# A graph layer with gathered sums: two matrices for u, later first slots, and a reload of node numbers set apart

## The chip, the cores and the metric

The kernel runs on one core of a Trainium2 chip. The metric is the device time of one launch in microseconds (us), lower is better. A core has five engines with a queue of instructions each: TensorE (PE, matmuls, with its weight loads shown as PEld), VectorE (DVE), ScalarE (ACT), GpSimd (POOL) and SyncE (SP, here used to start DMAs). Each engine works through its queue in order and waits on semaphores for the others. ACT, POOL and SP start DMAs, which run on the core's 16 DMA engines.

## The reference

A relational graph layer on N = 1250 nodes with D = 1024 features, E = 20000 edges of R = 8 types, with a normalization before it and a gate behind it:

```python
h = jnp.maximum(_layernorm(x, axis=-1), 0.0)
# u = _rgcn(h, edge_index, edge_type, weight, root, bias):
msgs = h[src]
out = h @ root + bias
for r in range(8):
    mask = (edge_type == r).astype(h.dtype)
    sums = jax.ops.segment_sum(msgs * mask[:, None], dst, num_segments=n)
    cnt = jax.ops.segment_sum(mask, dst, num_segments=n)
    mean = sums / jnp.maximum(cnt, 1.0)[:, None]
    out = out + mean @ weight[r]
u = out
z = jnp.concatenate([u, h], axis=1) @ w_gate + b_gate
out = x + jnp.tanh(u) * z + h * (1.0 - z)
```

## The kernel before

**The order of the mathematics.** The kernel multiplies first and sums over edges afterwards: for every edge type r it computes y_r = h @ weight[r] and writes it to DRAM. A node's u is then a weighted sum of rows of y, one row per incoming edge, the weight being one over the count of that node's edges of that type.

**TensorE's work.** Eleven matrices stand in the list `mats`: the eight weights, `root`, and the two halves of `w_gate`. `steps` runs over (s, i): s is the matrix, i one of five pairs of 128-row blocks of nodes (`NP` = 5, `ND` = 10 blocks). A step multiplies a pair of blocks with a matrix by Strassen's scheme (Winograd's form), so that seven products take the place of eight: function `product` (L270) with `step` (L361). From s = 1 on, one of the products of pairs 0 to 3 is itself taken apart once more (class `Second`, L178; its matmuls are the 128x256 ones of L209). The products' results are moved out of PSUM by ACT (copies, L303 to L337) and DVE (additions, L296, L304, L240), into `row` tiles of which there are four; SP stores the finished rows (L379), which frees the tile.

**Work beside the products.** After each of the seven products `product` calls `between(j)`. There a generator of other work is moved on: the function `spread` (L1058) deals `total` calls of a generator evenly over `parts` places, and `beside` (L1099) runs the steps up to matrix `last` with such a generator beside them. All engines' queues are in the order in which this Python code issues instructions; nothing reorders them afterwards. A DVE instruction of the side work thus stands in DVE's queue ahead of the row additions of the next product.

**Three groups of edges.** The types are cut in three groups, `R0 = (0, 3, 6, 8)`. Group g's sums begin when its y matrices (`y[g]`) are complete, and run beside two later matrices: group one beside s = 4 and 5, group two beside 6 and 7, group three beside 8 (`root`) and 9. In each group the nodes are sorted by their count of edges, and cut in ten blocks d of 128; `K[g][d]` says how many edges ("slots") the block's nodes have at most: 75, 75 and 52 slots per group. The sorted order is kept in `node[:, g, d]` (node numbers), and `idx[:, g, d, k]` is the row of y that slot k takes.

**One slot** is `add_slot` (L1003): POOL gathers 128 rows of y by `idx` into one of four `got` tiles (L1006), and DVE adds them, weighted, to the block's tile u (L1014; L1012 for the first slot of group one).

**One group** is the generator `edges` (L1026). `new_u` (L1018) makes a block's tile u; from the second group on it gathers u's state out of the DRAM matrix `u_dram` by node number (L462), because the groups have different orders. The tile of the next block is made at the second slot of the present one, after the finished block before it has been handed to `to`. For groups one and two `to` is `u_back` (L1051), which scatters u into `u_dram` by node number (`to_rows`, L466 to L471; the scatters of one group are declared independent of each other, as their rows differ). For group three it is a store to `last_dram` by SP (L1207), and for its last four blocks (`held`, L1281) u stays in SBUF. There is one matrix `u_dram`; a gather from it waits until every scatter into it that was issued earlier has landed.

**Node numbers of a group** come from `rows_and_weights` (L496): ten scatters of 4-byte values to `node_dram[g]` (L499), a reload of them as `node[:, g]` (L508), the keys `node_key` by a POOL addition (L509), and ten gathers of `idx` rows by key (L462). For group one it runs at once; for groups two and three it is a generator (`other_groups`, L1112) moved on at every second call of group one's slots. `weights(g)` computes the slots' weights on DVE (L486 to L491) after that.

**Overflow.** Nodes with more edges than slots are handled in a branch that these inputs do not enter: `passes_needed` (L1073) computes the flag beside group two, all engines load it (L1144) and branch (L1146) between the second and the third group.

Of the kernel before, what the change touches and what calls it, by code (L numbers as in the profile page):

```python
# [9 lines left out]
F32 = mybir.dt.float32  # L10
# [3 lines left out]
OP = mybir.AluOpType  # L14
# [5 lines left out]
def tile_rgcn_highway(  # L20
# [31 lines left out]
    nc = tc.nc  # L52
# [4 lines left out]
    N, D = x.shape  # L57
# [6 lines left out]
    ND = -(-N // P)  # L64
    NP = ND // 2
    NCH = -(-E // P)
    EL = E - (NCH - 1) * P
    G = 3
    R0 = (0, 3, 6, R)
# [5 lines left out]
    KEYS = ND * P  # L75
# [2 lines left out]
    FAR = 1 << 20  # L78
    CG = 4
    GOT = 4  # L80

    A11, A12, A22, S1, S2, S3, S4 = range(7)
    A21 = S3
# [17 lines left out]
    psum = ctx.enter_context(tc.tile_pool(name="psum", bufs=1, space=bass.MemoryType.PSUM))  # L101

    h_dram = dram.tile([N, D], F32, name="h_dram")
    u_dram = dram.tile([N, D], F32, name="u_dram")
    hr_dram = dram.tile([N, D], F32, name="hr_dram")
    z_dram = dram.tile([N, D], F32, name="z_dram")
    xh_dram = dram.tile([N, D], F32, name="xh_dram")
# [352 lines left out]
    def rows_of(to, of, at):  # L460

        nc.gpsimd.indirect_dma_start(  # L462
            out=to, out_offset=None, in_=of,
            in_offset=bass.IndirectOffsetOnAxis(ap=at, axis=0))

    def to_rows(of, frm, at, group):  # L466
        nc.gpsimd.memset(apart, 0.0)
        ins = nc.gpsimd.indirect_dma_start(  # L468
            out=of, out_offset=bass.IndirectOffsetOnAxis(ap=at, axis=0), in_=frm, in_offset=None)
        tc.declare_no_dep(ins.ins, query=no_wait, group=group, reason="rows differ")  # L470
        tc.add_to_no_dep_group(group, ins.ins)  # L471
# [24 lines left out]
    def rows_and_weights(g):  # L496

        for d in range(ND):
            ins = nc.gpsimd.indirect_dma_start(  # L499
                out=node_dram[g][:, :],  # L500
                out_offset=bass.IndirectOffsetOnAxis(ap=pos_i[:, g, d:d + 1], axis=0),
                in_=ids[:, d:d + 1], in_offset=None,
                bounds_check=KEYS - 1, oob_is_err=False)
            tc.declare_no_dep(ins.ins, query=no_wait, group="nodes", reason="places differ")
            tc.add_to_no_dep_group("nodes", ins.ins)
            if d % 2:
                yield
        nc.gpsimd.dma_start(node[:, g, :], node_dram[g].rearrange("(d p) o -> p (d o)", p=P))  # L508
        nc.gpsimd.tensor_single_scalar(node_key[:, g, :], node[:, g, :], g * KEYS, op=OP.add)  # L509
        yield  # L510
        yield
        for d in range(ND):
            rows_of(idx[:, g, d, :], table_rows, node_key[:, g, d:d + 1])
            if d % 2:
                yield

    with ExitStack() as early:
# [20 lines left out]
        class Normed:  # L538
# [13 lines left out]
            def spread(self):  # L552
                n = self.n
                nc.vector.bn_aggr(self.mv[:n], self.st[:n].rearrange("p a b -> p (a b)"))
                nc.scalar.activation(self.sd[:n], self.mv[:n, 1:2], AF.Sqrt, bias=eps[:n])
# [425 lines left out]
    with ExitStack() as edges_part:  # L981
# [41 lines left out]
                rows_of(u[:n], of[:, :], node[:n, g, d:d + 1])  # L1023
            return u

        def edges(g, blocks, to):  # L1026


            of = u_dram if g else None
            ahead = new_u(blocks[0], of, g)  # L1030
            behind = []

            def leave():
                while behind:
                    to(*behind.pop())

            for d in blocks:
                u = ahead
                last = K[g][d] - 1
                for k in range(last + 1):  # L1040
                    add_slot(u, g, d, k, idx[:, g], w_of[:, g], first=g == 0 and k == 0)
                    if k == min(1, last):
                        leave()
                        if d != blocks[-1]:
                            ahead = new_u(d + 1, of, g)
                    yield
                behind.append((d, u))
            leave()
            yield

        def u_back(g):  # L1051
            def to(d, u):
                n = nrows(d)
                to_rows(u_dram[:, :], u[:n], node[:n, g, d:d + 1], f"u{g}")

            return to

# [41 lines left out]
        def beside(e, total, s, i, last):  # L1099


            between = spread(e, total, 7 * ((last - s) * NP + NP - i))
            while s <= last:
                step(s, i, between)
                s, i = next(steps, (NM, 0))
            return s, i
# [26 lines left out]
        def with_passes(e):  # L1133
            passes = passes_needed()
            for _ in e:
                next(passes, None)
                yield

        for g in range(1, G - 1):
            e = edges(g, range(ND), u_back(g))  # L1140
            s, i = beside(with_passes(e) if g == G - 2 else e, sum(K[g]) + 1, s, i, R0[g + 2] - 1)


        passes = nc.values_load(n_pass[0:1, 0:1], min_val=0, max_val=E // MORE,  # L1144
# [1 line left out]
        with tc.If(passes > 0):  # L1146
            def further(g, d, ks, at, w):
                n = nrows(d)
                u = upool.tile([P, D], F32, name="u")
                rows_of(u[:n], u_dram[:, :], node[:n, g, d:d + 1])  # L1150
                for k in ks:
                    add_slot(u, g, d, k, at, w)
                nc.gpsimd.indirect_dma_start(
                    out=u_dram[:, :],
                    out_offset=bass.IndirectOffsetOnAxis(ap=node[:n, g, d:d + 1], axis=0),
                    in_=u[:n], in_offset=None)

            for g in range(G):
                for d in range(ND):
                    if K[g][d] < SLOTS:  # L1160
                        further(g, d, range(K[g][d], SLOTS), idx[:, g], w_of[:, g])
            scratch = got()
            used = [0]

            def part_of(n):
                used[0] += n
                return scratch[:, used[0] - n:used[0]]

            done = rank
            nc.vector.tensor_single_scalar(done, rank, float(-SLOTS), op=OP.add)  # L1170
            far_more = part_of(G * ND * MORE).bitcast(I32)
            nc.gpsimd.memset(far_more, FAR)
            under, where, where_i = part_of(NCH), part_of(NCH), part_of(NCH).bitcast(I32)
            at_more = part_of(ND * MORE).bitcast(I32).rearrange("p (d k) -> p d k", k=MORE)
            w_more, t_more = [part_of(ND * MORE).rearrange("p (d k) -> p d k", k=MORE)
                              for _ in range(2)]
            with tc.For_i(0, passes, 1):
                nc.gpsimd.dma_start(table_more.rearrange("(p f) o -> p (f o)", p=P), far_more)
                nc.vector.tensor_single_scalar(under, done, 0.0, op=OP.is_lt)
                nc.vector.tensor_single_scalar(where, done, float(MORE), op=OP.is_ge)  # L1180
                nc.vector.tensor_add(under, under, where)
                nc.vector.scalar_tensor_tensor(where, key_col, float(MORE), done,
                                               op0=OP.mult, op1=OP.add)
                nc.vector.scalar_tensor_tensor(where, under, float(FAR), where,
                                               op0=OP.mult, op1=OP.add)
                nc.vector.tensor_scalar_max(where_i, where, 0.0)
                for c in range(NCH):
                    n = nedges(c)
                    nc.gpsimd.indirect_dma_start(
                        out=table_more[:, :],  # L1190
                        out_offset=bass.IndirectOffsetOnAxis(ap=where_i[:n, c:c + 1], axis=0),
                        in_=row_col[:n, c:c + 1], in_offset=None,
                        bounds_check=G * KEYS * MORE - 1, oob_is_err=False)
                for g in range(G):
                    slot_rows(g, more_rows, at_more)
                    slot_weights(g, at_more, w_more, t_more, drc)
                    for d in range(ND):
                        further(g, d, range(MORE), at_more, w_more)
                nc.vector.tensor_single_scalar(done, done, float(-MORE), op=OP.add)
# [16 lines left out]
        def in_turn(*es):  # L1216
            for e in es:
                yield from e
# [62 lines left out]
        def held():  # L1281

            new, old = [], []
            for _ in edges(LG, range(HELD), lambda d, u: new.append(add_hr(d, u))):
                yield
                for add in old:
                    add()
                old, new[:] = new[:], []
            for add in old + new:
                add()  # L1290

        late = edges(LG, range(HELD, ND), to_last)
        between = spread(in_turn(late, held()), sum(K[LG]) + 2, 7 * ((NM - 2 - s) * NP + NP - i))
        while s < NM - 1:
            def beside_h(j):
                between(j)
# [69 lines left out]
```

## Time and profile before

| | |
|---|---|
| Median of 3 runs | 1399.93 us (1399.35 to 1403.1) |
| The profiled execution's own time | 1399.42 us |
| Its span | 1397.6 us |
| DVE L1014, slot additions | 192 of 1282 ns, 245.7 us |
| POOL L1006, slot gathers | 202 of 1238 ns, 250.2 us |
| POOL L468, scatters to u_dram | 20, median 1035 ns |
| POOL L462, gathers from u_dram | 20, median 957 ns |
| DMA queue of POOL's indirect transfers | 128.60 MB, 30.0% of 16 engines |
| TensorE's mean granted clock | 0.99 |

How to read the lines in what follows. A line of the timeline gives start and duration in us, the engine, the source line, the operation, the tiles written and read, and how many instructions are merged in it; the bracket is the time that the engine sat idle before it and what ended that. A line of the list of waits gives who waited for whom, the total in us and how often. A DMA's line on POOL is only its issue; the transfer lands later (a scatter to u_dram or a gather from it 4.1 to 6.5 us after, 5.7 in the median). In the slices, the span is cut in 40 equal parts of 35 us, and a digit is the busy share in tenths.

### The profile page before, as it was taken

What the parts mean: (1) busy time and instruction counts of PE and PEld (TensorE: products, weight loads), DVE (VectorE), ACT (ScalarE), POOL (GpSimd) and SP (SyncE); (2) the same over time, 40 slices, a digit from 0 to 9 for tenths busy, and PEclk for the clock granted to TensorE, in tenths of its full rate; (3) what the DMA queues carried; (4) which work ended last, traced back from release to release, by engine and by line L of the source; (5) the groups of instructions that cost most, each with busy time, mean ns of one, the idle gap of its engine ahead of it and who ended that gap; (6) DMA issues with size and microseconds to landing.
All of it is one profiled execution on the core that took longest, in us unless ns stands there. A gap on an engine that the chain in (4) does not pass through costs nothing.

```text
span 1397.6 us, 12703 instructions
## 1 busy us (share of the span) xinstructions
PE 1358.3 (97%) x3786; PEld 658.3 (47%) x3786; DVE 928.8 (66%) x1842; ACT 365.2 (26%) x793; POOL 630.6 (45%) x567
## 2 busy tenths in 40 slices
PE   7999999999999999999999999999779999999997
PEld 4444455445445545544454554454334445544443
DVE  6947977886869646556566655664367474567985
ACT  3335666566521111111111111111011111121220
POOL 0004655665543615656664543544345334335641
PEclk9999999999999999999999999999899999999999
DMA  8764545754742465398698638778749653577861
GB/s 312 267 200 112 124 125 151 167 121 118 170 144 64 127 181 119 95 305 178 208 311 286 226 108 290 258 258 288 246 165 311 237 179 110 188 275 233 290 202 57
DMA packets 110011, 272.78 MB, mean 195 GB/s; under 512 B 25906, under 2 KB 27936, under 8 KB 109808
## 3 DMA queue, kind: packets, MB, share of 16 engines
q0 software_dynamic: 48864, 128.60, 30.0%
q1 hardware_dynamic: 45232, 111.86, 25.9%
q10 hardware_dynamic: 15840, 31.46, 6.8%
q8 instruction: 30, 0.49, 0.1%
q14 instruction: 45, 0.37, 0.1%
HBM read 214.20 MB, written 80.65 MB: 211 GB/s over the span
## 4 chain that ended last, share of the span: by engine, by line
PE 54%; issue 14%; DMA 12%; DVE 9%; POOL 5%; ACT 1%; POOLq 0%; DVEq 0%; ACTq 0%
PE ps L282 48%; DMA got<-y,idx 8%; PE ps L209 6%; DMA u<-u_dram,node 2%; DVE u L1014 2%; POOL got L1006 1%; POOL got L462 1%; DMA w<-in_L_gnn_weight_dram 1%; POOL u_dram L468 1%; DVE junk L818 0%; DVE w L172 0%; DMA got<-hr_dram,node 0%; DMA h_op<-z_dram,node 0%; DVE seen L758 0%; PE ps_n L753 0%
## 5 line engine op out<-in xcount | busy, mean ns | idle before, releaser
L282 PE MATMUL ps<-w,h_op 128*128 128x512 f32 x2800 | 1236.8, 596 | 19.8 <-DVE row L240 10.2
L282 PEld LDWEIGHTS ps<-w,h_op 128*128 128x128 f32 x2800 | 527.4, 191 | 627.0 <-issue 594.3
L1014 DVE SCALAR_TENSOR_TENSOR u<-got,w_of,u 128x1024 f32<-128x1024 f32 (+1 forms) x192 | 245.7, 1282 | 188.2 <-DMA got<-y,idx 178.3
L1006 POOL DMA_INDIRECT got<-y,idx x202 | 250.2, 1238 | 255.6 <-DVE u L1014 159.4
L832 POOL DMA_INDIRECT table<-row_col,at_i x157 | 176.8, 1126 | 149.6 <-DVE at_i L828 70.7
L304 DVE TENSOR_TENSOR row<-row,part 128x512 f32<-128x512 f32 x55 | 37.8, 688 | 94.1 <-ACT part L303 94.1
L337 ACT COPY row<-ps 128x512 f32<-128x512 f32 x50 | 29.2, 585 | 236.4 <-PE ps L282 230.7
L303 ACT COPY part<-ps 128x512 f32<-128x512 f32 x55 | 32.1, 584 | 181.6 <-PE ps L282 181.6
L311 ACT COPY row<-ps 128x512 f32<-128x512 f32 x55 | 32.1, 584 | 168.5 <-PE ps L282 162.7
L315 ACT COPY row<-ps 128x512 f32<-128x512 f32 x55 | 32.2, 585 | 163.2 <-PE ps L282 139.7
L296 DVE TENSOR_TENSOR row<-row,ps 128x512 f32<-128x512 f32 x55 | 37.6, 683 | 54.2 <-PE ps L282 45.0
L209 PE MATMUL ps<-w,w 128*128 128x256 f32 x288 | 71.5, 381 | 0.0
L319 ACT COPY row<-ps 128x512 f32<-128x512 f32 x55 | 32.2, 585 | 139.8 <-PE ps L282 139.8
L468 POOL DMA_INDIRECT u_dram<-u,node x20 | 29.4, 1471 | 77.4 <-DVE u L1014 77.2
L209 PEld LDWEIGHTS ps<-w,w 128*128 128x128 f32 x288 | 54.1, 190 | 19.0 <-issue 13.4
L818 DVE SCALAR_TENSOR_TENSOR junk<-k_bc,key_col,before 128x128 f32<-128x128 int32 x157 | 54.9, 350 | 4.2
L209 PE MATMUL ps<-w,h_op 128*128 128x256 f32 x216 | 56.3, 383 | 0.0
L499 POOL DMA_INDIRECT node_dram<-ids,pos_i x30 | 36.5, 1218 | 39.4 <-issue 38.6
L758 DVE TENSOR_TENSOR seen<-seen,ps_n 128x110 f32<-128x110 f32 x157 | 42.1, 268 | 16.7 <-PE ps_n L753 12.7
L209 PEld LDWEIGHTS ps<-w,h_op 128*128 128x128 f32 x216 | 40.1, 190 | 23.0 <-issue 19.1
L735 ACT ACTIVATE is_lo<-io,less_lo 128x128 bf16<-128x128 f32 x157 | 50.1, 390 | 0.8 <-DVE row L304 0.8
L886 DVE SCALAR_TENSOR_TENSOR junk<-v_bc,val,one 128x1280 bf16<-128x1280 f32 x30 | 46.5, 1550 | 4.1 <-DMA v_bc<-val_dram 3.3
(182 smaller groups left out, 947.4 us busy)
## 6 DMA issues: line engine op xcount, KB each, us to landing
y<-row SPq DMA_DIRECT2D x72, 512.0 KB
w<-in_L_gnn_weight_dram ACTq DMA_DIRECT2D x21, 1024.0 KB
w<-in_L_gnn_weight_dram SPq DMA_DIRECT2D x11, 1024.0 KB
k_bc<-keys_dram SPq DMA_DIRECT2D x39, 256.0 KB
l_bc<-los_dram SPq DMA_DIRECT2D x39, 256.0 KB
w<-in_L_gnn_w_gate_dram ACTq DMA_DIRECT2D x6, 1024.0 KB
h_dram<-h_op SPq DMA_DIRECT2D x9, 512.0 KB
hr_dram<-row SPq DMA_DIRECT2D x9, 512.0 KB
```

The lines of the kernel that those rows point to most:

```text
L209: nc.tensor.matmul(p, a[:, k, :], b[:, k, :], start=(fresh and k == 0), stop=(k == 1), skip_group_check=True)
L282: nc.tensor.matmul(b[:, at], aop[:, i, k, :], w.of[i][:, k, at], start=(fresh and k == 0), stop=(k == KQ - 1), skip_group_check=True)
L296: nc.vector.tensor_add(c12, c12, c)
L304: nc.vector.tensor_add(c22, c22, d)
L468: ins = nc.gpsimd.indirect_dma_start(out=of, out_offset=bass.IndirectOffsetOnAxis(ap=at, axis=0), in_=frm, in_offset=None)
L735: nc.scalar.activation(is_lo[:, i, :], io, AF.Abs, bias=less_lo[:, c0 + i:c0 + i + 1])
L758: nc.vector.tensor_add(seen[j][:, i, :], was, p[:, i, :])
L818: nc.vector.scalar_tensor_tensor(junk, o["k_bc"][:, i, :], key_col[:, c:c + 1], before, op0=OP.is_equal, op1=OP.mult, accum_out=rank[:, c: ...
L832: ins = nc.gpsimd.indirect_dma_start(out=table[:, :], out_offset=bass.IndirectOffsetOnAxis(ap=at_i[:n, i:i + 1], axis=0), in_=row_col[:n, ...
L886: nc.vector.scalar_tensor_tensor(junk, v_bc[:, g, :], val[:, c:c + 1], one.to_broadcast([P, KEYS]), op0=OP.is_gt, op1=OP.mult, accum_out=p ...
L1006: nc.gpsimd.indirect_dma_start(out=t[:n], out_offset=None, in_=y[g][:, :], in_offset=bass.IndirectOffsetOnAxis(ap=at[:n, d, k:k + 1], axis=0),
L1014: nc.vector.scalar_tensor_tensor(u[:n], t[:n], w, u[:n], op0=OP.mult, op1=OP.add)
```

## The change

It has three parts. u has two DRAM matrices: group one scatters into the first, group two gathers from the first and scatters into the second, group three gathers from the second (as does the overflow branch). In groups two and three the first gather of u is issued at the border (`next(e)` ahead of `beside` and `spread`), and the generator then passes over `LATE` = 4 calls before its first slot; the totals of calls rise accordingly (76 to 79 in group two, 54 to 58 in group three). In `rows_and_weights` one more call lies between the node scatters and the reload, and the keys are computed two calls after the reload, not right behind it.

```diff
     GOT = 4
+    LATE = 4
@@
-    u_dram = dram.tile([N, D], F32, name="u_dram")
+    u_dram = [dram.tile([N, D], F32, name=f"u_dram{g}") for g in range(2)]
@@ rows_and_weights
             if d % 2:
                 yield
+        yield
         nc.gpsimd.dma_start(node[:, g, :], node_dram[g].rearrange("(d p) o -> p (d o)", p=P))
-        nc.gpsimd.tensor_single_scalar(node_key[:, g, :], node[:, g, :], g * KEYS, op=OP.add)
         yield
         yield
+        nc.gpsimd.tensor_single_scalar(node_key[:, g, :], node[:, g, :], g * KEYS, op=OP.add)
@@ edges
-        def edges(g, blocks, to):
+        def edges(g, blocks, to, late=0):
-            of = u_dram if g else None
+            of = u_dram[g - 1] if g else None
             ahead = new_u(blocks[0], of, g)
             behind = []
+            for _ in range(late):
+                yield
@@ u_back
-                to_rows(u_dram[:, :], u[:n], node[:n, g, d:d + 1], f"u{g}")
+                to_rows(u_dram[g][:, :], u[:n], node[:n, g, d:d + 1], f"u{g}")
@@
         for g in range(1, G - 1):
-            e = edges(g, range(ND), u_back(g))
-            s, i = beside(with_passes(e) if g == G - 2 else e, sum(K[g]) + 1, s, i, R0[g + 2] - 1)
+            e = edges(g, range(ND), u_back(g), LATE)
+            e = with_passes(e) if g == G - 2 else e
+            next(e)
+            s, i = beside(e, sum(K[g]) + LATE, s, i, R0[g + 2] - 1)
@@ further (the overflow branch)
-                rows_of(u[:n], u_dram[:, :], node[:n, g, d:d + 1])
+                rows_of(u[:n], u_dram[-1][:, :], node[:n, g, d:d + 1])
...
-                    out=u_dram[:, :],
+                    out=u_dram[-1][:, :],
@@
-        late = edges(LG, range(HELD, ND), to_last)
-        between = spread(in_turn(late, held()), sum(K[LG]) + 2, 7 * ((NM - 2 - s) * NP + NP - i))
+        late = edges(LG, range(HELD, ND), to_last, LATE + 1)
+        next(late)
+        between = spread(in_turn(late, held()), sum(K[LG]) + 2 + LATE, 7 * ((NM - 2 - s) * NP + NP - i))
```

## The prediction

> **What bounds the kernel now.** I read first the busy shares and the 40 slices, then TensorE's timeline in order of time, then the other engines around its gaps.
>
> ```profile
> PE 1358.3 (97%) x3786; PEld 658.3 (47%) x3786; DVE 928.8 (66%) x1842; ACT 365.2 (26%) x793; POOL 630.6 (45%) x567
> PE   7999999999999999999999999999779999999997
> ```
>
> TensorE bounds it: only 1397.6 - 1358.3 = 39.3 us of the span are idle, and the slices show two of them, near 980 to 1050 us. The part that the diff touches runs from 483 us (first slot gather of the first group) to 1256 us (last of the third). In it TensorE's timeline has three gaps worth the name (start, length, count, idle before and its releaser):
>
> ```profile
> 670.22 5.40 PE L282 MATMUL ps<-w,h_op 128*128 128x512 f32 x8 [2.44 <-DVE row L240]
> 677.18 3.60 PE L282 MATMUL ps<-w,h_op 128*128 128x512 f32 x8
> ...
> 997.89 26.24 PE L282 MATMUL ps<-w,h_op 128*128 128x512 f32 x56 [9.25 <-ACT row L315]
> ...
> 1048.30 6.04 PE L282 MATMUL ps<-w,h_op 128*128 128x512 f32 x8 [7.76 <-DVE row L240]
> ```
>
> Call them A (670), B (998) and C (1048). After a gap eight matmuls take 5.40 or 6.04 us and not 3.60, so a gap costs more than its idle time. The full price comes from a place that recurs once per weight matrix, the run of 128x256 matmuls which starts at 547.99, 666.75, 789.91, 908.89, 1039.51 and 1168.63: the distances are 118.76, 123.16, 118.98, 130.62 and 129.12 us. Against the undisturbed 118.76, A costs 4.4, B 11.9 and C 10.4 us, 26.7 together. Nothing else in the touched part costs TensorE time, so 26.7 us is all that this change can win there.
>
> Who makes B? GpSimd (POOL) and VectorE (DVE) before it:
>
> ```profile
> 972.30 1.82 POOL L468 DMA_INDIRECT u_dram<-u,node  x1 [3.80 <-DVE u L1014]
> 980.68 0.95 POOL L462 DMA_INDIRECT u<-u_dram,node  x1 [6.56 <-DMA u_dram<-u,node]
> 981.94 1.00 POOL L1006 DMA_INDIRECT got<-y,idx  x1 [0.30 <-issue]
> ...
> 989.20 1.28 DVE L1014 SCALAR_TENSOR_TENSOR u<-got,w_of,u 128x1024 f32<-128x1024 f32 x1 [14.67 <-DMA got<-y,idx]
> 990.40 0.69 DVE L304 TENSOR_TENSOR row<-row,part 128x512 f32<-128x512 f32 x1
> ...
> 997.25 0.59 ACT L315 COPY row<-ps 128x512 f32<-128x512 f32 x1 [14.81 <-DMA y<-row]
> ```
>
> POOL scatters a block's u into u_dram, then may not gather the next block's u out of it until that scatter has landed. The slot gather at 981.94 is queued behind; its addition (L1014) stands in DVE's order ahead of the row additions L304 and L240; the store of those rows goes out at 992.64, its landing frees a row buffer for ACT at 997.25, and TensorE goes on at 997.89. In the list of waits the same pair is
>
> ```profile
> POOL u L462 <- DMA u_dram<-u,node: 38.1, 9, 8.1
> ```
>
> (total us, times, longest). C is the border of groups two and three: u gather at 1032.63, slot gathers at 1036.69, 1038.01 and 1040.58, and three additions that wait for them in front of L240:
>
> ```profile
> 1041.06 1.28 DVE L1014 SCALAR_TENSOR_TENSOR u<-got,w_of,u 128x1024 f32<-128x1024 f32 x1 [8.28 <-issue]
> 1046.63 1.28 DVE L1014 SCALAR_TENSOR_TENSOR u<-got,w_of,u 128x1024 f32<-128x1024 f32 x1 [1.96 <-DMA got<-y,idx]
> 1047.83 0.41 DVE L240 TENSOR_TENSOR row<-row,ps 128x256 f32<-128x256 f32 x1
> ```
>
> A: two slot gathers at 658.04 and 659.88 land at about 667.1, their additions start at 667.23, L240 follows at 669.75.
>
> **What the Trainium skill says.** "TensorE: Matmul & The Clock Gate", section "Part 1: The HAM clock gate": the clock gate idles at half rate and opens after about 3.4 us of sustained work. The trace agrees: 6.04 us for what takes 3.60. "DMA: Bandwidth & Descriptors", "Two DMAs through the same engine are not ordered": a DMA that reads what an earlier one wrote must wait for that one's semaphore. That is L462's wait, and the reason it can go only if reader and writer have different matrices. Same page, "Specifications": below 512 B a transfer is not at line rate. The trace agrees: from 660 to 663 us, with the 4-byte node scatters in flight, the DMA engines are fully taken and move 29 GB/s.
>
> **The change part by part.** Counted from the built program, no engine gains or loses an instruction (2,214 on DVE, 1,408 on POOL and so on, untaken branches included); only order and waits differ.
>
> *Two matrices.* In the second group the reads go to the first matrix and the scatters to the second. In the new waits, u gathers inside that group no longer wait for a scatter of their own group; what some keep is the wait for the DMA eight back. Nine waits, 38.1 us, leave POOL. Of that only B was on the path. Locally: after the scatter (972.30 + 1.82) and one issue step (0.31) the u gather starts at 974.43, 6.25 us earlier. If everything behind it shifts by 6.25, B's idle falls from 9.25 to 3.0 us, and with a cold start (2.6, from 11.86 - 9.25) B still costs 5.6: the lower bound of the gain is 6.3. Upstream, the u gather at 958.13 also waited (3.70 us), and additions at 965.83 waited 7.96 for gathers behind it. DVE can move up there until TensorE sets it (L247 at 970.41 needs matmuls that end at 967.97), another 2.4 us. 6.25 + 2.4 = 8.65 of 9.25; a remainder of 0.6 us should bring no cold start (that is an estimate: the nearest case, 0.14 us idle before 910.05, left its matrix at 118.98). I take the whole 11.9. What is late next: the scatter still stands between the slots on POOL and waits for DVE's last addition, so POOL then leads by two slots, not four. A slot comes every 118.76 x 2 / 76 = 3.1 us, so that lead covers about 6.2 us of the usual 6.0 us landing. DVE waits remain, but TensorE has borne a wait of 10.66 us (before 1010.14) without a gap.
>
> *Four calls on.* The first u gather goes out at the border, the slots' calls four later. At group three DVE's new order is weight sums, L240, L304, then the first addition, L296, the second. L240 no longer stands behind three additions; it can run when its matmuls end, about 1040.6. The next product (3.43) and its copy and L304 (0.59 + 0.69) end at 1045.3; the first slot, on POOL's unchanged times, had landed by 1041.06: 4.2 us to spare. C goes whole: 10.4. Its bounds: if POOL's restart after the branch (L1146 holds it until 1031.5) is 4 us worse, a few us of C return; above 10.4 nothing can be won. What it costs elsewhere: group two has 79 calls and not 76 in the same 70 places, group three 58 and not 54, so slots come 4% and 7% denser. DVE is 66% busy and POOL 45%, so this is hidden; without that cover it would be some 12 us of slots pushed past the end of the group. The 30 small operations of the overflow test (2.3 us together, 782.77 to 785.28) move ahead of the weight sums, in a stretch where DVE stood idle 7.58 us: nothing. SP's store of one finished block moves behind an hr store; no row store waits more.
>
> *Node numbers.* POOL's two waits in front of A (2.59 at 663.49, 4.39 at 668.91) go: four slot gathers now lie between scatters and reload, four more before the keys. But the late pair of gathers at 658.04 is issued ahead of those waits, behind a u scatter and two 4-byte scatters, and these stay. What helps is upstream: three and not four pairs of node scatters lie between the u scatters at 619.13 and 652.08, so POOL comes there up to 2.6 us earlier (two issues), about A's 2.44 us. Bounds: 0 (DVE, not POOL, is late there) and 4.4; below zero if the pair moved behind 659.88 delays the next slots, which had 4.49 us of wait without a gap, so no loss. I take half, 2.2.
>
> Sum: 11.9 + 10.4 + 2.2 = 24.5 us. Span 1397.6 - 24.5 = 1373.1; around the span lie 1399.42 - 1397.6 = 1.8, so 1374.9, say 1375.0. The profiled execution is 0.5 us below the median of 1399.93, less than the runs' spread (1399.35 to 1403.1).
>
> **The rivals.** *B is contention, not the wait.* Two 1 MB weight loads go out at 970.55 and 981.88; slot gathers could land as late as now because they share the DMA engines and follow a 512 KB scatter. For it: the scatter itself took 6 to 8 us. Against it: from 975 to 985 the DMA engines were only half taken. Then only C and half of A go: 1399.4 - 12.6 = 1386.8; with a half of B, about 1381.
>
> *Nothing gained.* The denser slots and the removed cover give back what B and C paid, or the branch at the border still holds the first slots: within 4 us of 1399.9.
>
> *Slower: unthrottled POOL crowds the DMA engines.* Without the waits, each of the nine block borders of group two has a 512 KB scatter, a 512 KB gather and slot gathers in flight at once, beside stores and weight loads. If a slot's landing grows past the 10 us that TensorE bears, each border makes a gap like A (4.4 us). Nine of them are 40, less the 22.3 won at B and C: 1399.4 + 17 = 1417; it decides from six borders on (26 us). For it: the DMA share is 0.7 to 1.0 in most of these slices. Against it: in the first group slot gathers follow the scatter with no such wait, at the same pace, and only A came of it.
>
> **How the numbers follow.** Forecast (B and C go, A between all and nothing: 1372.7 to 1377.1): 0.60. B in part or whole left (1380 to 1387): 0.23. Nothing gained: 0.07. Slower: 0.10. The range 1370 to 1388 takes in the first two, 0.83, with 2.7 us below for small waits that I don't see. About 0.3% (4.2 us) is what a measurement can tell from no change; so faster 0.83, same 0.07, slower 0.10.
>
> **What would show it.** In the profile after: no L462 waiting for a u_dram scatter inside group two, and the distances of the 128x256 runs near 119 us in all three disturbed matrices; B right if no ACT L315 waits for a y store near 985; C right if L240 at the third group's start follows its matmul and not an addition; A open, read from DVE's wait near 667. Wrong if new gaps of 2 us or more stand at block borders, if slot gathers take over 10 us to land, or if TensorE's busy time, not its idle time, has changed.

## The result, and the profile after

| | before | after |
|---|---|---|
| Median | 1401.51 us (4 runs, 1399.35 to 1405.17) | 1379.52 us (4 runs, 1377.57 to 1388.04) |
| Ratio, 95% interval | | 0.9852 [0.9805, 0.99] |
| Profiled execution, its own time | 1399.42 us | 1378.6 us |
| Its span | 1397.6 us | 1376.8 us |
| TensorE busy, idle | 1358.3, 39.3 us | 1353.1, 23.7 us |
| Mean granted clock | 0.990 | 0.998 |

The change made the kernel 22.0 us faster in this measurement, where 24.5 were forecast. In two later ones, each on a chip of its own, the same kernel was 17.4 and 16.6 us faster than the kernel before (1386.15 against 1403.56, 1384.83 against 1401.47 us). As a ratio the forecast was 1375.0 / 1399.93 = 0.982. The interval above holds it; those of the two later measurements (full_again and full_third) begin at 0.984 and do not.

The profile's page of the kernel after shows the same bound as before, and the dip of the two slices near 980 to 1050 us is gone:

```profile
PE 1353.1 (98%) x3786; PEld 656.9 (48%) x3786; DVE 928.6 (67%) x1842; ACT 365.3 (27%) x793; POOL 632.6 (46%) x567
PE   7999999999999999999999999999999999999997
```

Between 540 and 1300 us, TensorE's timeline has one gap left. It is a new one; call it D:

```profile
750.00 25.97 PE L283 MATMUL ps<-w,h_op 128*128 128x512 f32 x56 [2.74 <-ACT row L316]
```

The marks that recur once per weight matrix (the run of 128x256 matmuls of the prediction, first mark at 547.99 before and 549.15 after) give the balance. I write for each matrix what it took beyond the undisturbed 118.76 us. Group one ends a little ahead of the third mark, so A and D lie in the second distance:

| distance between marks | before | after |
|---|---|---|
| second (A before, D after) | 123.16: 4.4 | 123.44: 4.7 |
| third | 118.98: 0.2 | 118.98: 0.2 |
| fourth (B) | 130.62: 11.9 | 118.75: 0 |
| fifth (C) | 129.12: 10.4 | 118.76: 0 |

So B and C are gone whole in this execution, and A's 4.4 us came back as D's 4.7. The part of the kernel ahead of the first mark, where the edges are sorted, ended 1.16 us later in this execution, and the stretch after the last mark is the same (228.96 against 228.97). The sum: -11.9 - 10.4 - 4.4 + 4.7 + 1.2 = -20.8, the difference of the spans.

In the list of waits of the kernel after (total us, times, longest), the nine waits of a u gather for a u scatter are down to one, and the longest wait of DVE for a slot gather is 7.1 us where it was 14.7 at B:

```profile
DVE u L1016 <- DMA got<-y,idx: 152.6, 60, 7.1
...
ACT row L316 <- DMA y<-row: 15.8, 3, 8.3
...
POOL u L463 <- DMA u_dram<-u,node: 3.5, 1, 3.5
```

The one that is left is the first gather of group two (771.75 us), which reads what group one has just scattered. It stood among the nine before (774.60, 3.18 us of wait). The other eight were waits inside group two, where a block's gather reads other rows than the scatter ahead of it writes; two matrices let those go. The experiments below agree: every further profile with two matrices has one such wait, of 3.2 to 4.2 us, and every one with a single matrix has nine.

Line numbers differ by one or two between the kernels: L1016 is the addition that was L1014, L463 the gather that was L462, L469 the scatter that was L468, L241 the row addition that was L240, L316 the copy that was L315. Some experiments add a few more lines.

**Where B was.** The same block border in the timeline of the kernel after, on POOL, DVE and ACT:

```profile
970.54 1.03 POOL L469 DMA_INDIRECT u_dram<-u,node  x1 [1.62 <-DVE u L1016]
...
971.87 0.96 POOL L463 DMA_INDIRECT u<-u_dram,node  x1 [0.30 <-issue]
973.13 1.00 POOL L1008 DMA_INDIRECT got<-y,idx  x1 [0.30 <-issue]
...
981.44 1.28 DVE L1016 SCALAR_TENSOR_TENSOR u<-got,w_of,u 128x1024 f32<-128x1024 f32 x1 [3.85 <-DMA got<-y,idx]
982.64 0.41 DVE L241 TENSOR_TENSOR row<-row,ps 128x256 f32<-128x256 f32 x1
...
987.85 0.59 ACT L316 COPY row<-ps 128x512 f32<-128x512 f32 x1 [4.38 <-DMA y<-row]
```

The u gather follows its scatter by one issue step, 0.30 us, where it had waited 6.56. ACT still waits for a row's store, 4.38 us and not 14.81, and TensorE does not notice.

**Where C was.** DVE at the border of groups two and three, after:

```profile
1021.85 0.41 DVE L241 TENSOR_TENSOR row<-row,ps 128x256 f32<-128x256 f32 x1
1022.18 0.68 DVE L305 TENSOR_TENSOR row<-row,part 128x512 f32<-128x512 f32 x1
1030.16 1.28 DVE L1016 SCALAR_TENSOR_TENSOR u<-got,w_of,u 128x1024 f32<-128x1024 f32 x1 [7.29 <-issue]
```

L241 runs 8.3 us ahead of the group's first addition. Before, its twin L240 stood behind three additions and ran at 1047.83.

**Where D comes from.** The kernel after ahead of 750.00, with DVE, SP's queue and ACT:

```profile
740.28 1.28 DVE L1016 SCALAR_TENSOR_TENSOR u<-got,w_of,u 128x1024 f32<-128x1024 f32 x1 [5.54 <-DMA got<-y,idx]
...
741.48 0.68 DVE L305 TENSOR_TENSOR row<-row,part 128x512 f32<-128x512 f32 x1
...
743.72 1.81 SPq L380 DMA_DIRECT2D y<-row  x3
...
749.37 0.59 ACT L316 COPY row<-ps 128x512 f32<-128x512 f32 x1 [8.30 <-DMA y<-row]
```

It is B's chain again (late slot, row additions behind it, late store, no row buffer for ACT), but in group one, where no u is gathered and so no wait for a scatter can be its cause. Before, L304 ran at 740.32. Counted from the first mark that is the same moment (192.33 us after it in both), but TensorE was 4.4 us further behind because of A, and no gap showed. So A seems to have hidden D in these two executions.

### The profile page after: what moved, and what is told of

It reads as the page before. It is cut to its first block, busy times and chain, and to the rows that moved or that the text cites. A ratio compares the mean times of both kernels' runs of the same rounds, so it can differ in the third digit from the quotient of the medians.

```text
span 1376.8 us, 12702 instructions
## 1 busy us (share of the span) xinstructions
PE 1353.1 (98%) x3786; PEld 656.9 (48%) x3786; DVE 928.6 (67%) x1842; ACT 365.3 (27%) x793; POOL 632.6 (46%) x567
## 4 chain that ended last, share of the span: by engine, by line
PE 70%; issue 8%; DVE 6%; DMA 6%; POOL 3%; ACT 1%; POOLq 0%; DVEq 0%; ACTq 0%
PE ps L283 62%; PE ps L210 7%; DMA got<-y,idx 4%; POOL got L1008 2%; DMA u_dram<-u,node 1%; DMA w<-in_L_gnn_weight_dram 1%; PE ps_n L755 0%; DVE seen L760 0%; DVE u L1016 0%; DVE junk L820 0%; DMA y<-row 0%; DMA u<-last_dram 0%; DMA got<-h_dram,node 0%; DVE row L1321 0%; DVE h_op L1257 0%
## 5 line engine op out<-in xcount | busy, mean ns | idle before, releaser
L1016 DVE SCALAR_TENSOR_TENSOR u<-got,w_of,u 128x1024 f32<-128x1024 f32 (+1 forms) x192 | 245.5, 1281 | 161.7 <-DMA got<-y,idx 152.6
L304 ACT COPY part<-ps 128x512 f32<-128x512 f32 x55 | 32.1, 584 | 181.4 <-PE ps L283 181.4
L316 ACT COPY row<-ps 128x512 f32<-128x512 f32 x55 | 32.2, 585 | 141.6 <-PE ps L283 124.6
L469 POOL DMA_INDIRECT u_dram<-u,node x20 | 26.4, 1318 | 73.2 <-DVE u L1016 67.1
L500 POOL DMA_INDIRECT node_dram<-ids,pos_i x30 | 38.6, 1285 | 39.3 <-issue 38.7
```

Of the source, the lines that this page charges most:

```text
L500: ins = nc.gpsimd.indirect_dma_start(out=node_dram[g][:, :], out_offset=bass.IndirectOffsetOnAxis(ap=pos_i[:, g, d:d + 1], axis=0), in_=id ...
L1016: nc.vector.scalar_tensor_tensor(u[:n], t[:n], w, u[:n], op0=OP.mult, op1=OP.add)
```

## Experiments

Twelve experiments: nine variants, one of which was run a second time (e5_third, then third_again), and the change itself twice more (full_again, full_third). Each computes the whole reference. They ran in three groups, each on a chip of its own with its own runs of the kernel before: medians 1396.98 (43 runs, 1388.66 to 1408.88), 1403.56 (11 runs) and 1401.47 us (11 runs). Ratios are against those.

The theory at the start: each part removes the gap that it was priced for. The rivals: B is contention and not the wait; the denser slots give back what C wins; the node part moves group one's delay without removing it.

**One part at a time.** First the node part alone: node numbers reloaded one call later, keys two calls later, and nothing else.

```diff
             if d % 2:
                 yield
+        yield
         nc.gpsimd.dma_start(node[:, g, :], ...)
-        nc.gpsimd.tensor_single_scalar(node_key[:, g, :], ...)
         yield
         yield
+        nc.gpsimd.tensor_single_scalar(node_key[:, g, :], ...)
```

> Only the third part: reload and keys of node numbers apart from their scatters; u_dram one matrix, no late slots. Theory 'the gather stream paces group one' (removing the wait at A lets TensorE run ahead of the slot gathers, and it meets them again at D, about 80 us later): gap A gone, a gap D of 2 to 5 us near 750 in its place, B and C as before, time within 2 us of before. Theory 'A is a gain of its own and D a chance of one execution': A gone, no D, 4.4 us less than before (ratio 0.997).

Measured: 1397.0 us over 22 runs, ratio 0.9989 [0.9967, 1.0012]. Its TensorE timeline has no A at 670, but D, B and C:

```profile
748.91 24.30 PE L282 MATMUL ps<-w,h_op 128*128 128x512 f32 x56 [2.47 <-ACT row L315]
992.34 26.52 PE L282 MATMUL ps<-w,h_op 128*128 128x512 f32 x56 [5.43 <-ACT row L315]
1040.96 5.50 PE L282 MATMUL ps<-w,h_op 128*128 128x512 f32 x8 [5.70 <-DVE row L240]
```

The part does what was said at A and yields nothing that can be measured; the interval still has room for the 2.2 us that were forecast (0.9984). This profile also shows how much one execution can differ from another: B and C cost 7.9 and 7.8 us here (distances of 126.67 and 126.52) and not 11.9 and 10.4, though this part lies in group one, and D costs 2.7 (121.49).

The two matrices alone:

```diff
-    u_dram = dram.tile([N, D], F32, name="u_dram")
+    u_dram = [dram.tile([N, D], F32, name=f"u_dram{g}") for g in range(2)]
...
-            of = u_dram if g else None
+            of = u_dram[g - 1] if g else None
...
-                to_rows(u_dram[:, :], u[:n], node[:n, g, d:d + 1], f"u{g}")
+                to_rows(u_dram[g][:, :], u[:n], node[:n, g, d:d + 1], f"u{g}")
```

> Only the first part: two matrices for u. Theory 'the scatter-to-gather wait makes B': B (11.9 us) gone, A and C stay: 1388 us, ratio 0.9915. Theory 'B is contention with the weight loads': B stays in most of its length, ratio over 0.997. Either way no u gather in group two waits for a u scatter of the same group.

Measured: 1383.28 us, ratio 0.9893 [0.9863, 0.9924], some 15 us. TensorE's timeline:

```profile
670.23 3.70 PE L282 MATMUL ps<-w,h_op 128*128 128x512 f32 x8 [2.48 <-DVE row L240]
...
1031.99 6.41 PE L282 MATMUL ps<-w,h_op 128*128 128x512 f32 x8 [3.76 <-DVE row L240]
```

A is there, B is not (fourth distance 118.76), and C is smaller: the fifth distance is 125.49, which is 6.7 us beyond the undisturbed one and not 10.4. B's 11.9 and 3.7 of C make 15.6, close to the runs' 15; but C was 7.8 in the kernel with the node part alone too, so it is not shown that two matrices made C smaller. That B was contention and not the wait is refuted: the wait went, and B with it.

The late slots alone, with one matrix:

```diff
-        def edges(g, blocks, to):
+        def edges(g, blocks, to, late=0):
+            for _ in range(late):
+                yield
...
-            e = edges(g, range(ND), u_back(g))
-            s, i = beside(with_passes(e) if g == G - 2 else e, sum(K[g]) + 1, s, i, R0[g + 2] - 1)
+            e = edges(g, range(ND), u_back(g), LATE)
+            e = with_passes(e) if g == G - 2 else e
+            next(e)
+            s, i = beside(e, sum(K[g]) + LATE, s, i, R0[g + 2] - 1)
...
-        late = edges(LG, range(HELD, ND), to_last)
+        late = edges(LG, range(HELD, ND), to_last, LATE + 1)
+        next(late)
```

> Only the second part: first u gather at the border, slots four calls later; one u matrix. Theory 'C is three additions queued ahead of a row addition': C (10.4 us) gone, A and B stay: about 1389 us, ratio 0.9925. Theory 'the denser slots give it back': B grows or new gaps appear in group two, ratio over 0.997.

Measured: 1396.06 us over 22 runs, ratio 0.9983 [0.9964, 1.0001]. C is gone (fifth distance 118.76), and B has grown. The timeline around 1000 us on POOL, DVE, ACT and TensorE:

```profile
982.93 1.82 POOL L469 DMA_INDIRECT u_dram<-u,node  x1 [1.62 <-DVE u L1015]
991.93 0.95 POOL L463 DMA_INDIRECT u<-u_dram,node  x1 [7.19 <-DMA u_dram<-u,node]
998.50 1.29 DVE L1015 SCALAR_TENSOR_TENSOR u<-got,w_of,u 128x1024 f32<-128x1024 f32 x1 [11.95 <-DMA got<-y,idx]
...
1004.00 0.58 ACT L316 COPY row<-ps 128x512 f32<-128x512 f32 x1 [21.68 <-DMA y<-row]
...
1004.64 26.02 PE L283 MATMUL ps<-w,h_op 128*128 128x512 f32 x56 [16.12 <-ACT row L316]
```

The gap at B is 16.12 us of idle time and not 9.25; the fourth distance is 136.86, 18.1 beyond the undisturbed one. What C gave (10.4), B took back in good part (18.1 - 11.9 = 6.2). The row store that ends the wait at B goes out 91.0 us after the fourth mark (1000.14 less 909.18), where it was 83.8 us before (992.64 less 908.89). The second rival held here: the slots gave back most of what C won. Two things in this part could do that: the delay in group two, which pushes 76 calls into what is left of its places, or the one in group three, which begins only behind B.

**Two parts together.** First and second, without the node part.

> First and second part without the third. Theory 'the gather stream paces group one': A there, no D, B and C gone: the time of the full change within 2 us (about 1377 to 1379). Theory 'A is a gain of its own': 4.4 us slower than the full change when that one has no D, that is about the same now, but the full change would then show D in few executions. The gap times near 670 and 750 tell.

Measured: 1384.41 us, ratio 0.9886 [0.9848, 0.9924]. Its first theory was a time level with the full change, 1377 to 1379 us, with A and without D. C is gone and B nearly (1.69 us idle at 998.17, a fourth distance of 120.72), but group one lost 10.9 us in this profile (second distance 129.69): a small A (0.56 us idle at 670.04), 4.00 us at 706.17, and 2.26 at 756.78, where D stands. So D comes without the node part too, and A does not always hide it. The interval does not part this kernel from the two matrices alone.

**The delay in one group only.** The late slots kept for group three, and group two as before: once with one matrix and the node part as before, once with the rest of the change.

```diff
-            e = edges(g, range(ND), u_back(g), LATE)
+            e = edges(g, range(ND), u_back(g))
             e = with_passes(e) if g == G - 2 else e
-            next(e)
-            s, i = beside(e, sum(K[g]) + LATE, s, i, R0[g + 2] - 1)
+            s, i = beside(e, sum(K[g]) + 1, s, i, R0[g + 2] - 1)
```

With one matrix:

> One u matrix, node numbers as before, late slots in group three alone. Theory 'the delay in group two is what grew B to 16 us in the run with both delays': C gone, B as before (9 us idle): about 10 us less than before, ratio 0.9925. Theory 'B's length is a matter of the single execution': B between 5 and 16 us, the ratio near that of the run with both delays (0.998).

Measured: 1391.86 us, ratio 0.9912 [0.9883, 0.9941]. C is gone (fifth distance 118.75), and B stays below its old size (fourth distance 126.52, the row store 77.3 us after the fourth mark):

```profile
998.13 26.05 PE L283 MATMUL ps<-w,h_op 128*128 128x512 f32 x56 [5.74 <-ACT row L316]
```

The interval lies apart from that of the same part with the delay in both groups (0.9983 [0.9964, 1.0001], on another chip): the delay in group three is worth about 0.9%, and the one in group two costs most of that when the u gathers wait. My step that the denser slots are hidden is wrong for group two. Whether the slots' later start or their density does it was not tried apart.

With the whole change, beside a second run of the change itself:

> The full change once more, beside the others of this call. Theory 'group one is paced by its gathers': before 790 us a gap at A or at D (2 to 4 us each) in this execution too, none at B and C; about 0.987 of before. Theory 'D was a chance': no gap at either place, 0.983.

> The full change, but late slots in group three alone (group two begins as before, 76 calls). Theory 'C is won by the delay at group three, and the delay in group two only packs its slots nearer to B': C and B gone, the time of the full change or 1 to 2 us less. Theory 'group two needs its delay': a gap or a lagging row addition near 790 us, 2 us or more over the full change.

Measured on one chip: 1386.15 us, 0.9872 [0.9844, 0.9899], for the change as it is, and 1380.45 us, 0.9829 [0.9801, 0.9857], with the delay in group three only. The intervals overlap, so I ran both again, on another chip:

> The full change a third time, on the same chip as third_again. 0.985 to 0.987 against before, 0.004 above third_again if the delay in group two costs; level with it if not. The trace shows gaps in group one alone (A or D), and the matrix distances of groups two and three at 118.8 to 119.

> The whole change, but with the delay in group three only. If the delay in group two costs what it packs together: again some 0.004 (5 us) below the full change on this chip, and no gap in the matrices of group two and three. Rival, the difference seen last time (0.9829 against 0.9872) was the spread of runs: within 0.002 of the full change.

Measured: 1384.83 us, 0.9865 [0.9837, 0.9894], against 1381.22 us, 0.9854 [0.9828, 0.988]. Twice in the same direction, by 5.7 and 3.6 us, and not beyond the intervals in either case. The traces give a reason. Around B, the change as it is (run full_third) has

```profile
984.45 1.28 DVE L1016 SCALAR_TENSOR_TENSOR u<-got,w_of,u 128x1024 f32<-128x1024 f32 x1 [3.90 <-DMA got<-y,idx]
985.65 0.41 DVE L241 TENSOR_TENSOR row<-row,ps 128x256 f32<-128x256 f32 x1
...
986.09 2.07 SPq L380 DMA_DIRECT2D y<-row  x3
...
993.77 0.59 ACT L316 COPY row<-ps 128x512 f32<-128x512 f32 x1 [7.75 <-DMA y<-row]
```

and the one with the delay in group three only (run third_again) has

```profile
980.41 1.28 DVE L1016 SCALAR_TENSOR_TENSOR u<-got,w_of,u 128x1024 f32<-128x1024 f32 x1
981.60 0.42 DVE L241 TENSOR_TENSOR row<-row,ps 128x256 f32<-128x256 f32 x1
...
982.05 2.01 SPq L380 DMA_DIRECT2D y<-row  x3
```

The store that frees the row buffer goes out 4.0 us later where group two's slots began late, since the addition ahead of L241 does; TensorE itself is 1.1 us later there (marks at 912.87 and 911.73), so 2.9 us of that count against it. In full_third that left a gap of 2.19 us at 994.41 and a fourth distance of 122.91. Of the five profiles with two matrices and a delayed group two, three have such a gap at B (e4_two_late, full_third and e6_early, below). None of those with two matrices and an undelayed group two has one (e2_two, e5_third, third_again, e9_two_third, e8_early_third). The row store tells why: counted from the fourth mark of each profile it goes out after 71.8 to 73.8 us in the five with the delay and after 69.9 to 70.5 us in the five without, and the three gaps belong to the three latest stores (73.2, 73.7 and 73.8). That the delay in group two makes row stores late where B was is thus shown by all ten profiles; what it costs in time with two matrices is not settled, since the runs' intervals overlap.

**The node part, where B and C are gone.** The delay in group three only and two matrices, but the node numbers as before:

> Two matrices, and the late slots in group three only; the node numbers as before. The node part is worth nothing once group one is paced by its gathers: then this is level with the kernel that has it too (third_again), at a ratio of 0.983 +/- 0.003 against before, with gap A (2.5 us idle near 670) in the trace and a short D. Rival, the node part is worth its 4.4 us (0.3%) where B and C are gone: a ratio of 0.986, 0.003 above third_again, and group one's two matrices (starts of the first to the third) longer by 4 us.

Measured: 1380.39 us, 0.9844 [0.9823, 0.9865], level with third_again at 0.9854, which has the node part too. Without it, TensorE's timeline in group one has A and a short gap 34 us behind it:

```profile
673.09 3.70 PE L283 MATMUL ps<-w,h_op 128*128 128x512 f32 x8 [2.47 <-DVE row L241]
706.99 1.13 PE L210 MATMUL ps<-w,w 128*128 128x256 f32 x4 [1.77 <-DVE w L203]
```

With it, in third_again, neither, but D:

```profile
751.38 26.00 PE L283 MATMUL ps<-w,h_op 128*128 128x512 f32 x56 [3.79 <-ACT row L316]
```

The second distance is 123.54 without and 124.51 with the node part. It is the same over all profiles with the small scatters among group one's slots: what the second distance has beyond 118.76 is 2.7 to 9.1 us in the six with the node part (median 5.6) and 3.9 to 10.9 in the six without it (median 4.2). That the part is worth its 4.4 us is not borne out anywhere; in full_again even A is not quite gone (0.36 us idle at 672.02, 1.75 at 705.90) and D stands beside it.

**What stretches group one.** Twenty 4-byte scatters of node numbers (ten each for groups two and three) stand between group one's slot gathers. I moved them ahead of group one's slots, in one row, first with the change as it is. The generator of the node part is shorter by them, so its reload, keys and idx gathers also come earlier:

```diff
-    def rows_and_weights(g):
+    def node_numbers(g):
         for d in range(ND):
...
-        yield
+
+    def rows_and_weights(g):
+
         nc.gpsimd.dma_start(node[:, g, :], node_dram[g]...)
@@ order, once a group's positions are known
+                    for _ in node_numbers(g):
+                        pass
```

> The full change, and the 20 scatters of 4-byte node numbers of groups two and three issued before group one's slots begin, where POOL is idle for about 33 us; reload, keys and idx gathers stay beside group one. Theory 'the 4-byte scatters hold up the slot gathers behind them, and this makes A and D': both gone, 3 to 5 us less than the full change. Theory 'group one is paced by slot gathers and weight loads alone': a gap at A or D stays, the time within 1 us of the full change.

Measured: 1388.67 us, 0.9887 [0.986, 0.9914]. A and D are both gone, and the second distance is 118.76 for the first time. But the time did not fall, because a new gap stands at 514.79, ahead of the first mark, and a small one at B. SP's queue and TensorE there:

```profile
498.84 11.23 SPq L380 DMA_DIRECT2D y<-row  x3
```

```profile
514.79 30.48 PE L283 MATMUL ps<-w,h_op 128*128 128x512 f32 x64 [3.93 <-issue]
...
998.69 24.30 PE L283 MATMUL ps<-w,h_op 128*128 128x512 f32 x56 [2.20 <-ACT row L316]
```

The 20 scatters are issued from 488 to 518 us; three row stores take 11.23 us to go out beside them, and the matrix that ends at the first mark takes 125.7 us, 6.9 too many. That the scatters hold up the stores is likely from this and not shown: the profile does not say what TensorE waited for at 514.79. The same with the delay in group three only:

> The delay in group three only, and the 20 scatters of 4 bytes ahead of group one's slots, in one row. The scatters are what stretches group one: the two matrices of group one at 118.8 each, but a gap near 514, where the scatters stand before the y stores (498.8 took 11.2 us in the earlier trace), so the sum is level with third_again, within 0.003. Rival, the gap near 514 was chance: the span is 4 to 5 us shorter than that of third_again (0.980).

Measured: 1373.97 us (1371.26 to 1375.07), 0.9802 [0.978, 0.9824]. This is the fastest kernel of the study. Without the move it is third_again, on the same chip: 1381.22 us (1374.71 to 1384.43), 0.9854 [0.9828, 0.988], so the move is worth some 7 us there, and the intervals just lie apart. Here my theory fell and its rival held: no gap near 514, and all five distances are 118.75 to 118.98. The row stores went out faster:

```profile
493.27 6.13 SPq L380 DMA_DIRECT2D y<-row  x3
```

In the waits between 548 and 790 us of the kernel after the change, and of this one, DVE's addition reads

```profile
DVE u L1016 <- DMA got<-y,idx: 79.0, 30, 6.2
```

```profile
DVE u L1020 <- DMA got<-y,idx: 56.3, 28, 7.9
```

which is 22.7 us less waiting for slots. And group one's blocks are finished earlier. Their third and fourth scatters to u_dram, after the change and here, are

```profile
651.50 2.83 POOL L469 DMA_INDIRECT u_dram<-u,node  x1 [2.50 <-DVE u L1016]
...
678.89 1.29 POOL L469 DMA_INDIRECT u_dram<-u,node  x1 [4.36 <-DVE u L1016]
```

```profile
645.09 2.83 POOL L469 DMA_INDIRECT u_dram<-u,node  x1 [2.02 <-DVE u L1020]
663.70 1.03 POOL L469 DMA_INDIRECT u_dram<-u,node  x1 [1.68 <-DVE u L1020]
```

At the fourth block group one is 15.2 us further back where the small scatters stand among its slots (14.2 counted from TensorE's marks at 667.91 and 666.90). The second distance tells the same across the study: 2.7 to 10.9 us too long in all 12 profiles (before and after among them) with the scatters among group one's slots, 0.0 in the two without. That A and D come of the node work of groups two and three as it stands among group one's slots is shown. That it is the scatters, and not what moved with them, is likely: up to the fourth block group one has had 10 idx gathers and 20 scatters after the change, 20 idx gathers and no scatter in e8_early_third, and is further on. But group three's idx gathers, between A and D after the change (685 to 711 us), also lie ahead of both here (600 to 628), so for D they remain a rival. By which of the scatters' costs, POOL's issue time (about 1 us each) or the DMA engines' time, was not tried apart.

Open: e6_early and e8_early_third are the same program up to the end of group one, and only the first, on another chip, had the gap at 514. I have no run that tells whether the chip or chance made it.

## Why the prediction was right, and where it was not

*Two matrices, 11.9 us.* Right in mechanism, and in size within what the runs can tell: alone the part is worth 1.07% [0.76, 1.37], 10.6 to 19 us, and B's matrix is undisturbed. Eight waits went, not nine; the one at the head of group two could not go, as it guards rows that group one has just written. The remainder of 0.6 us that I feared at B did not show in the first profile. I read the wait by the wrong rule, though. "Two DMAs through the same engine are not ordered" (the Trainium skill, "DMA: Bandwidth & Descriptors") speaks of a DMA that reads what an earlier one wrote. That fits the wait that stayed. Inside group two the rows read and the rows written differ, and the wait stood there only because both were one matrix.

*Four calls on, 10.4 us.* C went whole, as worked out: L240's twin now runs straight after the weight sums. The place that I took for it (when its matmuls end, about 1040.6 on the old clock) was too late, since these had ended before the weight sums did; the error only added cover. What was wrong is the cost beside it. I put "slots come 4% and 7% denser" at nothing, because DVE was 66% busy and POOL 45%. These are averages over the span. What matters at B is how far one slot gather is ahead of one row addition, and the delay in group two takes some of that: with two matrices its row store there goes out 1.3 to 3.9 us later than without the delay. With one matrix that ate most of C's gain (0.9983 where the delay in group three alone gave 0.9912); with two it leaves 0 to 4 us at B in single profiles.

*Node numbers, 2.2 us.* This is the step that failed. A went whole in the first profile, yet no gain of the part can be measured (0.9989 [0.9967, 1.0012] alone, and 0.9844 without it against 0.9854 with it), and group one's two matrices are no shorter with it than without (median excess 5.6 against 4.2 us). I priced the gap and not what sets group one's pace: the slot gathers run late beside the node work of the next groups, which the change left among them. With A gone, TensorE reached the next late slot sooner and waited there, 2.74 us at D. My bounds for it, 0 to 4.4, held the answer; the wrong thought was to take half, because "What is late next" was asked for B and not for A.

*The sum.* In the profiled pair it comes out term by term: 24.5, less the 2.2 of the node part, less 0.3 by which D costs more than A, less 1.2 ahead of the first mark, is the 20.8 between the spans. That the first measurement came so near is partly luck: its profile has no gap at B, where full_third has one, and the later two gave 17.4 and 16.6 us for the same kernel.

*The rivals.* Contention at B: refuted by the two matrices alone. Unthrottled POOL crowding the DMA engines: its sign came in part. I had named a landing of slot gathers over 10 us, and from 790 to 1020 us the longest took 12.2 us after the change and 9.0 before (medians 6.2 and 6.0). But no border of group two made a gap in that profile, and the gaps of about 2 us in three later ones stand at B alone; nothing like one at each of nine borders. Nothing gained: not refuted for two of the three parts when each is made alone, and false for the whole.

*The spread.* I took 0.3% for what a measurement can tell. The kernel before ran from 1388.66 to 1408.88 us over 43 runs on one chip, 1.5%, and the changed one from 1375.28 to 1389.92 over 16 runs. The profiles show one place where that comes from: the second distance alone varies from 123.44 to 127.83 between three profiles of the same changed kernel. So the forecast of 1375 was met by the best of these runs and missed by the medians, 1379.52, 1386.15 and 1384.83.

## What to carry to other kernels

A gap's price is what it costs TensorE only if the work behind it can be early too: before counting the gain, look for the next place where the same late stream (here the slot gathers of one group) meets TensorE. A delay that clears a border makes what follows later and denser; give it only to the stage whose border needs it. And ask where a few small scattered writes stand among a stream of gathers: moving 20 of them ahead of it was worth some 7 us here on one chip, while on another a gap that cost 6.9 us appeared where they went.

## What the runs showed of the hardware

Small gaps may or may not cost the clock. Here, idle times of TensorE and what came behind them, with the granted clock that the profile shows there:

| run, time | idle, us | matmuls behind it | granted clock behind it |
|---|---|---|---|
| full_third, 994.41 | 2.19 | 56 in 26.00 us | 0.84 for 1.6 us, then 0.58 for 3.5 us, then 1.00 |
| e6_early, 998.69 | 2.20 | 56 in 24.30 us | 1.00 |
| before, 670.22 (A) | 2.44 | 8 in 5.40 us | 0.58 for 3.4 us |
| e1_node, 748.91 (D) | 2.47 | 56 in 24.30 us | 1.00 |
| e9_two_third, 673.09 (A) | 2.47 | 8 in 3.70 us | 1.00 |
| after, 750.00 (D) | 2.74 | 56 in 25.97 us | 0.50 for 3.4 us, then 1.00 |

So near 2.2 to 2.5 us it falls either way. When it falls badly, the clock is at half for about 3.4 us, which costs half of that, the 1.7 us between 24.30 and 26.00; it need not begin with the first matmul behind the gap, as the mean of 0.84 in full_third's first 1.6 us shows. What decides is not shown. The Trainium skill, "TensorE: Matmul & The Clock Gate", section "Part 1: The HAM clock gate", has the clock go cold, to half rate, after at least one idle window of about 3.4 us. The half rate agrees with the 0.50 at 750.00; for the idle time, shorter ones were enough here, and the measurement decides.
